# A perceiver block on one core: the context tile's conversion stands behind the key eviction, and the key norm's product behind the next slot's first key products

## The chip, the cores and the metric

The kernel runs on one core of a Trainium2 chip. A core has five engines, each with its own in-order instruction stream: TensorE (PE, matrix products into PSUM), VectorE (DVE), ScalarE (ACT), GpSimd (POOL) and SyncE (SP, which only issues DMAs here). ScalarE also issues DMAs, in the order of its own stream. The metric is the device time in microseconds of one execution. The kernel before took 2119.9 us (median of three runs, 2117.38 to 2125.94).

## What is computed

Eight sequences of 64 tokens with 512 features attend to themselves and, in a cross attention, to a context of 1601 rows of 512 features each. Then follow a sparse attention over the 64 tokens and a feed-forward layer with ternary weights. The change touches the cross attention, whose part of the reference is:

```python
kvx = jnp.einsum('bsi,oi->bso', cond, w_kv_x)          # cond: (8, 1601, 512)
kx, vx = jnp.split(kvx, 2, axis=-1)
kx = _ln(kx.reshape(b, sc, g, d), kxln_w, kxln_b)      # 8 groups, d = 128
vx = vx.reshape(b, sc, g, d)
xout = _gqa(qx, kx, vx).reshape(b, s, nh * d)          # softmax(q k / sqrt(d)) v
```

Keys are thus a product of the context with a weight, normalised over the 128 features of each group and each context row.

## The kernel before

The cross attention is cut into 16 works: 8 sequences times 2 halves of the key groups (4 groups each). A work's context of 1601 rows is cut into 13 tiles of 128 rows (the last has 65), and the tiles into 6 chunks, of two tiles each and the last of three. One turn of the main loop (line 1208, variable g) is a slot. It does a step for one tile in each of several stages, which lag behind each other: a tile is loaded and converted at slot g, its chunk's keys are made 2 slots later (KEYS), the inverse norms are fetched 4 slots later (SPREAD), the scores are made 5 later (SCORES), and probabilities and the weighted sum of the context about 20 later (LAG). So while one work is weighed, the next one's keys are made. 208 slots hold the whole cross attention; other work (projections, self attention, weights, the sparse attention) is pumped in between as a background, with lower priority.

The code is traced in the order in which Python runs it. A scheduler then sets the order of each engine's stream from priorities (earlier in the program is more urgent) and its own estimate of when operands are ready. `tc.issue_after(x)` adds the condition that whatever the block traces on x's engine stands behind x in that engine's stream. It is an order, not a wait, and touches no other engine.

Products are made in pairs of a rounded part and a rest: hi and lo of every operand, three products each. The steps that matter here, for one slot:

- **turned** (line 556): SP loads a transposed context tile cTr (256 KB, L565); ScalarE converts it to cThi (L569); GpSimd takes the difference to cTlo (L570). An odd last tile (65 rows) gets a zero column first, by a GpSimd memset (L567). cTr shares its three buffers (tag "raw") with cr, the untransposed tile of the weighing stage.
- **keys** (line 572): 24 products kx (L588) for two groups of a chunk, 12 for each; ScalarE evicts them twice, the squares ksq (L595) and the scaled keys kthi (L596); VectorE transposes the squares (ksqt, L598), makes the rest ktlo (L599) and reduces the squares to kms (L600). A chunk's four groups take two slots (three for the last chunk).
- **norm** (line 604), once a chunk: a small product kz (L610) gathers kms over partitions into a PSUM bank; VectorE makes kown (L612) and kxv (L614); GpSimd raises to the power -0.5 (L616); VectorE transposes (krt, L618); SP stores 16 KB to DRAM (keyd, L620).
- **spread** (line 622): ScalarE's queue loads keyd back, broadcast to all partitions, into S (512 KB, 642 KB for the last chunk, L626).
- **scores** (line 628): products of queries and keys (L645) into PSUM, and VectorE multiplies them by S and takes the maximum (L649, written as S and cmx in the profile).
- **probs_t, context, weigh**: transposes pt (L677), their halves phi (ScalarE, L687) and plo (VectorE, L688), the context's halves chi (L717) and clo (L721), and 12 products acc (L740 to L742) into the sums U, which ut evicts at a work's end (L748).

PSUM has three banks of the pool that kz, the scores and pt share ("m"), four for the sums U and one for the background; while the sums run, kx takes its bank from the first pool too.

In the order before, a slot traces `turned` in front of `keys`, so conversion has the higher priority. The norm is traced at the slot's end, and its product stands behind `keyed[0]`, the slot's last key or weighing product:

```python
        if 0 <= gK < NA and LAST[kK]:
            with tc.issue_after(keyed[0].ins):
                work[nK].norm(JOBS[kK][0])
```

Of the kernel before, what the change touches and what calls it, by code (L numbers as in the profile page):

```python
# [16 lines left out]
AF = mybir.ActivationFunctionType  # L17
# [4 lines left out]
P = 128  # L22
H = 512
NIC = 4
# [37 lines left out]
def tile_perceiver(ctx: ExitStack, tc: tile.TileContext, t: dict):  # L62
    nc = tc.nc
    V, A, GP, PE = nc.vector, nc.scalar, nc.gpsimd, nc.tensor
# [16 lines left out]
    def nm(s):  # L81
        uid[0] += 1
        return f"{s}_{uid[0]}"

    def ctile(shape, dt, tag):
        return const.tile(shape, dt, tag=tag, name=tag)

    def sm(tag, k=1, dt=F32, bufs=None):
        kw = {} if bufs is None else {"bufs": bufs}
        return small.tile([P, k], dt, tag=tag, name=nm(tag), **kw)  # L90
# [8 lines left out]
    def kxp(tag="kx"):  # L99


        if lane["late"] is not None:
            return lane["late"]
        return accp(tag) if lane["wide"] else mainp(tag)

    def accp(tag="acc"):
        return pacc.tile([P, 512], F32, tag="acc", name=nm(tag))
# [32 lines left out]
    def v3(ap, g):  # L140
        return ap.rearrange("p (g k) -> p g k", g=g)
# [4 lines left out]
    class Late:  # L146
# [13 lines left out]
        ps = staticmethod(lambda tag="b": kxp())  # L160
# [67 lines left out]
    zeros = ctile([P, 1], F32, "zeros")  # L228
# [36 lines left out]
    hw = {"qx": qwb[:, 0:1], "q": qwb[:, 2:3], "k": at["k_norms"][:, 0:1], "kx": at["k_norms"][:, 2:3]}  # L265
# [262 lines left out]
    paced = [None]  # L528
    keyed = [None]
    turn = [None]  # L530
    pin = [None]

    class Cross:
# [22 lines left out]
        def turned(self, tt):  # L556

            t0, n = TT[tt]
            ci = CHUNK_OF[tt]
            o = t0 - TT[CHUNKS[ci][0]][0]  # L560
            if ci not in self.ct:
                self.ct[ci] = [mp.tile([P, NIC, CTW], F32R, tag=x, name=nm(x), bufs=2) for x in ("cThi", "cTlo")]
            chi, clo = self.ct[ci]
            raw = mp.tile([P, NIC, P], F32, tag="raw", name=nm("cTr"), bufs=3)
            paced[0] = nc.sync.dma_start(raw[:, :, :n], t["ctxT"][self.b].rearrange("(c p) k -> p c k", p=P)[:, :, t0:t0 + n])  # L565
            if n & 1:
                GP.memset(raw[:, :, n:n + 1], 0.0)  # L567
                n += 1
            A.copy(chi[:, :, o:o + n], raw[:, :, :n])  # L569
            GP.tensor_tensor(clo[:, :, o:o + n], raw[:, :, :n], chi[:, :, o:o + n].bitcast(F32), ALU.subtract)  # L570

        def keys(self, ci, gs):

            cw = sum(TT[tt][1] for tt in CHUNKS[ci])
            N = cw + (cw & 1)
            nj = (N + 31) // 32
            W = nj * 32
            chi, clo = self.ct[ci]
            if ci not in self.kt:
                self.kt[ci] = [mp.tile([P, HG, KTW], F32R, tag="kt" + x, name=nm("kt" + x), bufs=2) for x in ("hi", "lo")]  # L580
                self.ms[ci] = sm("kms", HG * NRM, bufs=2)
            hi, lo = self.kt[ci]
            ps = kxp()
            for i, g in enumerate(gs):
                k = 0
                for st, mv in ((self.wk[0], chi), (self.wk[1], chi), (self.wk[0], clo)):
                    for ic in range(NIC):
                        self.mm = PE.matmul(ps[:, i * N:(i + 1) * N], lhsT=st[:, ic, g * P:(g + 1) * P], rhs=mv[:, ic, :N], start=k == 0, stop=k == 11)  # L588
                        k += 1
            g0, g1, ng = gs[0], gs[-1] + 1, len(gs)  # L590
            sq = mp.tile([P, 512], F32, tag="kn", name=nm("ksq"), bufs=3)
            if W > N:
                for i in range(ng):
                    A.copy(sq[:, i * W + N:(i + 1) * W], zeros.to_broadcast([P, W - N]))
            A.activation(v3(sq[:, :ng * W], ng)[:, :, :N], v3(ps[:, :ng * N], ng), AF.Square, scale=1.0 / math.sqrt(D))  # L595
            turn[0] = A.activation(hi[:, g0:g1, :N], v3(ps[:, :ng * N], ng), AF.Copy, scale=hw["kx"])  # L596
            sqt = mp.tile([P, 512], F32, tag="kn", name=nm("ksqt"), bufs=3)
            V.transpose(sqt[:, :ng * W], sq[:, :ng * W])  # L598
            V.scalar_tensor_tensor(lo[:, g0:g1, :N], v3(ps[:, :ng * N], ng), hw["kx"], hi[:, g0:g1, :N].bitcast(F32), ALU.mult, ALU.subtract)  # L599
            pin[0] = V.tensor_reduce(self.ms[ci][:, g0 * nj:g1 * nj], sqt[:, :ng * W].rearrange("p (x a) -> p x a", a=32), AX.X, ALU.add)  # L600
            if g1 == HG:
                self.ct.pop(ci)
# [122 lines left out]
        def weigh(self, tt):  # L725

            t0, n = TT[tt]
            if tt == 0:
                self.U = [accp() for _ in range(NIC)]
            phi, plo = self.pp.pop(tt)  # L730
            chi, clo = self.cc.pop(tt)
            last = tt == len(TT) - 1
            for ic in range(NIC):
                s = slice(ic * P, (ic + 1) * P)
                if last:

                    PE.matmul(self.U[ic], lhsT=chi[:, s], rhs=phi, start=False, stop=False)
                    PE.matmul(self.U[ic], lhsT=clo[:S + 3, s], rhs=plo[:S + 3], start=False, stop=True)
                    continue
                PE.matmul(self.U[ic], lhsT=chi[:n, s], rhs=phi[:n], start=tt == 0, stop=False)  # L740
                PE.matmul(self.U[ic], lhsT=chi[:n, s], rhs=plo[:n], start=False, stop=False)  # L741
                keyed[0] = PE.matmul(self.U[ic], lhsT=clo[:n, s], rhs=phi[:n], start=False, stop=False)  # L742

        def weighed(self):
            self.ut = []
# [25 lines left out]
    def last_context():  # L771
        raw = load(mp.tile([P, 512], F32, tag="raw", name=nm("cr"), bufs=3)[:NB], t["ctx"][:, SC - 1, :])
        hi = mp.tile([P, 512], F32R, tag="chi", name=nm("chi"), bufs=2)
        lo = mp.tile([P, 512], F32R, tag="clo", name=nm("clo"), bufs=2)
        A.copy(hi[:NB], raw)
        V.tensor_tensor(lo[:NB], raw, hi[:NB].bitcast(F32), ALU.subtract)
        for b in range(NB):
            for r, x in enumerate((hi, hi, lo)):
                nc.sync.dma_start(codd[b][r:r + 1], x[b:b + 1].bitcast(F32))
# [411 lines left out]
    NT = len(TT)  # L1191
    TURN = {tt: (tt,) for tt in range(NT - 2)}
    TURN[NT - 2] = NT - 2, NT - 1
    JOBS = [(ci, [(2 * i, 2 * i + 1)]) for ci in range(NCH - 1) for i in range(2)]
    LAST = [i % 2 == 1 and i < 2 * (NCH - 1) or i == NT - 1 for i in range(NT)]
    JOBS += [(NCH - 1, x) for x in ([(0,)], [(1,)], [(2,), (3,)])]
    work = [Cross(b, half) for half in range(2) for b in range(NB)]
    NA = NT * len(work)
# [9 lines left out]
    for g in range(NA + LAG + 3):  # L1208
        nA, kA = divmod(g, NT)
        gK = g - KEYS  # L1210
        nK, kK = divmod(gK, NT)
# [36 lines left out]
                    w.exps(0, 0, 2)  # L1248
        if g == LAG - 4:
            last_context()  # L1250
        if g < NA:
            for tt in TURN.get(kA, ()):
                work[nA].turned(tt)
        if 0 <= gK < NA:
            ci, gs = JOBS[kK]
            for x in gs:
                work[nK].keys(ci, x)
            keyed[0] = work[nK].mm
        if g == 0:
            bgA.pump(ALL)  # L1260
        if g == 2:
# [33 lines left out]
        if 0 <= e < NA:  # L1295
            nE, kE = divmod(e, NT)
            work[nE].weigh(kE)
            if kE == NT - 1:
                work[nE].weighed()
        if 0 <= gK < NA and LAST[kK]:  # L1300
            with tc.issue_after(keyed[0].ins):
                work[nK].norm(JOBS[kK][0])
        for bg, q in ((bgA, PACE[g >= LATER]), (bgC, PACE[1]), (bgB, TERNARY_PACE if g < NA + FFN_AT else 0)):
            n = int((g + 1) * q) - int(g * q)

# [81 lines left out]
```

## Time and profile before

| what | value |
|---|---|
| median of three runs | 2119.9 us |
| profiled execution, whole | 2135.21 us |
| its span, first to last instruction | 2133.4 us |
| granted TensorE clock, mean | 0.952 |
| DMA, mean over the span | 190 GB/s |
| TensorE busy 150 to 600 / 600 to 1200 / 1200 to 1800 us | 422.51 / 551.39 / 557.23 us |
| VectorE busy in the same stretches | 336.91 / 409.34 / 372.83 us |
| ScalarE busy in the same stretches | 274.13 / 294.90 / 295.71 us |
| key products (L588), all three kinds | 4608, of some 290 ns each as recorded |
| weighing products (L740 to L742) | 2304, of some 400 ns each as recorded |
| conversions cThi (L569) / differences cTlo (L570) | 208 of 622 / 1195 ns (medians) |

Products overlap: one is recorded with its fill and drain, and the next begins before it ends, so a busy time is a union and the mean of one is longer than its share. A wait is told as the engine's idle time just before an instruction, with the one whose end released it. In the timeline each row has the start, the duration, the engine and line, what is written and read, and in brackets an idle time before it.

### The profile page before, as it was taken

Reading aid. Unit: us, or ns where it says so; the run is one execution under the profiler, and the core shown is the slowest. Engines: PE = TensorE matmul, PEld = TensorE weight load, DVE = VectorE, ACT = ScalarE, POOL = GpSimd, SP = SyncE. Lnnn points to the kernel's source line nnn. Section 1 sums busy time; section 2 is a strip of 40 time slices with the busy share of each in tenths; the row PEclk is TensorE's granted clock in tenths of the full one; section 3 lists DMA queues with packets and bytes.
Section 4 is the critical chain, followed back from the end, with each engine's and each line's share of the span. In section 5 each row is a group of like instructions: output and inputs, shape, how many; then the busy total and the mean of one; then the engine's idle time right before and its main releaser. Section 6 shows DMA issues by size and latency. Waiting matters only on the chain. (4 is left out here: it accounts for less than half of the span.)

```text
span 2133.4 us, 35936 instructions
## 1 busy us (share of the span) xinstructions
PE 1931.0 (91%) x12181; PEld 1702.1 (80%) x12181; DVE 1410.9 (66%) x3769; ACT 1107.7 (52%) x2612; POOL 563.3 (26%) x503
## 2 busy tenths in 40 slices
PE   5789999998999899998989999999989989997998
PEld 5678888888988788887878888888778778874766
DVE  7768787767787577676665556566674765565465
ACT  5456656555655455454434444445644644454554
POOL 5232323322222222212121222222232222210132
PEclk9789999999999999999999999999999999998989
DMA  6566575676565665788776676778556535572425
GB/s 194 141 175 191 153 198 160 194 244 188 161 189 155 209 206 167 226 261 263 246 230 224 218 255 211 250 214 274 170 160 202 163 115 165 157 228 83 142 72 166
DMA packets 361032, 406.31 MB, mean 190 GB/s; under 512 B 45696, under 2 KB 255744, under 8 KB 360848
## 3 DMA queue, kind: packets, MB, share of 16 engines
q1 hardware_dynamic: 310160, 351.54, 51.6%
q10 hardware_dynamic: 50688, 52.47, 10.4%
q8 instruction: 96, 1.57, 0.3%
q14 instruction: 88, 0.72, 0.1%
HBM read 336.40 MB, written 67.26 MB: 189 GB/s over the span
## 5 line engine op out<-in xcount | busy, mean ns | idle before, releaser
L570 POOL TENSOR_TENSOR cTlo<-cTr,cThi 128x512 fp32r<-128x512 f32 (+1 forms) x208 | 251.1, 1215 | 988.6 <-ACT cThi L569 856.9
L741 PE MATMUL acc<-plo,chi 128*128 128x512 f32 x768 | 306.6, 401 | 0.3 <-DVE plo L688 0.3
L742 PE MATMUL acc<-phi,clo 128*128 128x512 f32 x768 | 303.1, 397 | 0.2 <-DMA clo<-clod 0.2
L598 DVE STREAM_TRANSPOSE ksqt<-ksq 128x512 f32<-128x512 f32 (+1 forms) x224 | 147.8, 660 | 220.2 <-ACT ksq L595 219.6
L588 PE MATMUL kx<-cThi,wkhi 128*128 128x256 f32 (+1 forms) x1536 | 274.2, 299 | 5.8 <-DVE m1y L458 2.6
L588 PE MATMUL kx<-cThi,wklo 128*128 128x256 f32 (+1 forms) x1536 | 262.5, 292 | 0.0
L588 PE MATMUL kx<-cTlo,wkhi 128*128 128x256 f32 (+1 forms) x1536 | 261.4, 290 | 0.0
L740 PE MATMUL acc<-phi,chi 128*128 128x512 f32 x768 | 236.2, 412 | 18.8 <-ACT phi L687 18.6
L595 ACT ACTIVATE ksq<-kx 128x512 f32<-128x512 f32 (+1 forms) x224 | 123.7, 552 | 240.9 <-PE kx L588 235.5
L588 PEld LDWEIGHTS kx<-cThi,wkhi 128*128 128x128 f32 x1536 | 230.9, 196 | 21.7 <-DVE m1y L458 3.9
L569 ACT CAST cThi<-cTr 128x512 fp32r<-128x512 f32 (+1 forms) x208 | 122.8, 606 | 220.5 <-DMA cTr<-in_ctxT 145.1
L588 PEld LDWEIGHTS kx<-cThi,wklo 128*128 128x128 f32 x1536 | 224.3, 195 | 4.4 <-issue 3.3
L588 PEld LDWEIGHTS kx<-cTlo,wkhi 128*128 128x128 f32 x1536 | 221.6, 193 | 2.1 <-issue 0.8
L616 POOL TENSOR_TENSOR spread<-kxv,mhalf 128x8 f32<-128x8 f32 x96 | 172.0, 1792 | 185.3 <-DVE kxv L614 162.1
L665 ACT ACTIVATE S<-S,cnm 128x256 f32<-128x256 f32 (+1 forms) x384 | 196.7, 519 | 43.7 <-DVE cnm L660 43.7
L649 DVE CUSTOM_DVE_ANT_0 S<-s,S 128x256 f32<-128x256 f32 (+1 forms) x384 | 152.0, 427 | 68.7 <-DMA S<-keyd 36.5
L717 ACT CAST chi<-cr 128x512 fp32r<-128x512 f32 x192 | 119.1, 620 | 143.5 <-PE acc L741 82.5
L740 PEld LDWEIGHTS acc<-phi,chi 128*128 128x128 f32 x768 | 140.1, 195 | 47.7 <-ACT phi L687 23.7
L741 PEld LDWEIGHTS acc<-plo,chi 128*128 128x128 f32 x768 | 146.5, 191 | 30.2 <-issue 3.5
L742 PEld LDWEIGHTS acc<-phi,clo 128*128 128x128 f32 x768 | 145.7, 190 | 27.4 <-issue 0.8
L688 DVE TENSOR_TENSOR plo<-pt,phi 128x512 fp32r<-128x512 f32 x192 | 131.2, 684 | 53.1 <-ACT phi L687 52.2
L687 ACT CAST phi<-pt 128x512 fp32r<-128x512 f32 x192 | 112.5, 587 | 92.4 <-PE pt L677 92.0
(350 smaller groups left out, 3731.3 us busy)
## 6 DMA issues: line engine op xcount, KB each, us to landing
cTr<-in_ctxT SPq DMA_DIRECT2D x192, 256.0 KB
cr<-in_ctx SPq DMA_DIRECT2D x192, 256.0 KB
ws<-wpd SPq DMA_DIRECT2D x88, 512.0 KB
S<-keyd ACTq DMA_DIRECT2D x80, 512.0 KB
clod<-clo SPq DMA_DIRECT2D x96, 256.0 KB
clo<-clod SPq DMA_DIRECT2D x96, 256.0 KB
wv<-in_wkv SPq DMA_DIRECT2D x64, 256.0 KB
tern<-in_ffn_w SPq DMA_DIRECT2D x64, 256.0 KB
```

What stands on the lines that cost most here:

```text
L569: A.copy(chi[:, :, o:o + n], raw[:, :, :n])
L570: GP.tensor_tensor(clo[:, :, o:o + n], raw[:, :, :n], chi[:, :, o:o + n].bitcast(F32), ALU.subtract)
L588: self.mm = PE.matmul(ps[:, i * N:(i + 1) * N], lhsT=st[:, ic, g * P:(g + 1) * P], rhs=mv[:, ic, :N], start=k == 0, stop=k == 11)
L595: A.activation(v3(sq[:, :ng * W], ng)[:, :, :N], v3(ps[:, :ng * N], ng), AF.Square, scale=1.0 / math.sqrt(D))
L598: V.transpose(sqt[:, :ng * W], sq[:, :ng * W])
L616: GP.tensor_tensor(r[:, :nj], v[:, :nj], mhalf[:, :nj], ALU.pow)
L649: V.tensor_tensor_reduce(sc[:, g, :cw], ps[:, :cw], sc[:, g, :cw], 1.0, -3.0e38, ALU.mult, ALU.max, self.mx[:, g * NCH + ci:g * NCH + ci + 1])
L665: A.activation(self.S[ci][:, g, :cw], self.S[ci][:, g, :cw], AF.Exp, bias=self.nmx[:, g:g + 1], accum_out=self.su[:, g * NCH + ci:g * NCH ...
L688: V.tensor_tensor(lo[:n], pt[:n], hi[:n].bitcast(F32), ALU.subtract)
L740: PE.matmul(self.U[ic], lhsT=chi[:n, s], rhs=phi[:n], start=tt == 0, stop=False)
L741: PE.matmul(self.U[ic], lhsT=chi[:n, s], rhs=plo[:n], start=False, stop=False)
L742: keyed[0] = PE.matmul(self.U[ic], lhsT=clo[:n, s], rhs=phi[:n], start=False, stop=False)
```

## The change

Three things change. The zero column of an odd tile is written by ScalarE as a copy of a zero tile. `turned` is traced behind `keys` and the norm, and its ScalarE instructions stand behind `keyt[0]`, the slot's last key eviction (L596). The norm of a chunk is traced one slot later than before, right behind that slot's keys, and its product stands behind the first 12 of them (the last product of the first group); the weighing products no longer set `keyed[0]`.

```diff
             if n & 1:
-                GP.memset(raw[:, :, n:n + 1], 0.0)
+                A.copy(raw[:, :, n:n + 1], zeros.unsqueeze(1).to_broadcast([P, NIC, 1]))
...
-                        self.mm = PE.matmul(ps[:, i * N:(i + 1) * N], ...)
+                        mm = PE.matmul(ps[:, i * N:(i + 1) * N], ...)
                         k += 1
+                if i == 0:
+                    keyed[0] = mm
...
-            turn[0] = A.activation(hi[:, g0:g1, :N], v3(ps[:, :ng * N], ng), AF.Copy, scale=hw["kx"])
+            turn[0] = keyt[0] = A.activation(hi[:, g0:g1, :N], v3(ps[:, :ng * N], ng), AF.Copy, scale=hw["kx"])
...
-                keyed[0] = PE.matmul(self.U[ic], lhsT=clo[:n, s], rhs=phi[:n], start=False, stop=False)
+                PE.matmul(self.U[ic], lhsT=clo[:n, s], rhs=phi[:n], start=False, stop=False)
...
-        if g < NA:
-            for tt in TURN.get(kA, ()):
-                work[nA].turned(tt)
         if 0 <= gK < NA:
             ci, gs = JOBS[kK]
             for x in gs:
                 work[nK].keys(ci, x)
-            keyed[0] = work[nK].mm
+        if 0 <= gK - 1 < NA and LAST[(gK - 1) % NT]:
+            with tc.issue_after(keyed[0].ins):
+                work[(gK - 1) // NT].norm(JOBS[(gK - 1) % NT][0])
+        if g < NA:
+            for tt in TURN.get(kA, ()):
+                with tc.issue_after(keyt[0].ins) if keyt[0] is not None else nullcontext():
+                    work[nA].turned(tt)
...
-        if 0 <= gK < NA and LAST[kK]:
-            with tc.issue_after(keyed[0].ins):
-                work[nK].norm(JOBS[kK][0])
```

More of the change, by code (lines that the diff above doesn't have):

```diff
@@ L530, in tile_perceiver @@
     turn = [None]
+    keyt = [None]
     pin = [None]
@@ L587, in keys @@
                     for ic in range(NIC):
-                        self.mm = PE.matmul(ps[:, i * N:(i + 1) * N], lhsT=st[:, ic, g * P:(g + 1) * P], rhs=mv[:, ic, :N], start=k == 0, stop=k == 11)
+                        mm = PE.matmul(ps[:, i * N:(i + 1) * N], lhsT=st[:, ic, g * P:(g + 1) * P], rhs=mv[:, ic, :N], start=k == 0, stop=k == 11)
                         k += 1
+                if i == 0:
+                    keyed[0] = mm
             g0, g1, ng = gs[0], gs[-1] + 1, len(gs)
```

## The prediction

> **What bounds the kernel now.** I read the head of the page first, then the waits of each engine, then the order of time around one norm.
>
> ```profile
> span 2133.4 us, 35936 instructions
> PE 1931.0 (91%) x12181; PEld 1702.1 (80%) x12181; DVE 1410.9 (66%) x3769; ACT 1107.7 (52%) x2612; POOL 563.3 (26%) x503
> ```
>
> TensorE is busy for 91%; 202 us of the span are its gaps, and a change of order can only fill gaps or open new ones. Between 150 and 1915 us, where the slots run, the gaps sum to 1765 - 1641 = 124 us (busy time by stretches). The waits of all engines say who ended them (total us, times, longest):
>
> ```profile
> PE kz L610 <- DVE kms L600: 44.5, 30, 4.5
> PE acc L740 <- ACT phi L687: 18.6, 14, 3.0
> PE s L645 <- DVE kown L612: 10.2, 7, 3.2
> PE s L645 <- DVE cqb L652: 5.7, 6, 2.6
> ACT cThi L569 <- DMA cTr<-in_ctxT: 145.1, 67, 6.3
> POOL cTlo L570 <- ACT cThi L569: 856.9, 143, 19.4
> DVE S L649 <- DMA S<-keyd: 36.5, 16, 6.8
> ```
>
> The largest gap of TensorE is the norm's small product kz waiting for the reduction kms. The last row is the one to watch: even now the multiply of the scores by the inverse norms (S, L649) waits 16 times for its 512 KB to land. Its chain, in order of time, for one chunk:
>
> ```profile
> 664.24 0.31 PE L610 MATMUL kz<-kms,over 128*128 128x32 f32 x2
> 665.08 0.19 DVE L612 SCALAR_TENSOR_TENSOR kown<-kz,quad 128x32 f32<-128x32 f32 x1
> 665.30 0.22 DVE L614 TENSOR_REDUCE kxv<-kown 128x8 f32<-128x32 f32 x1
> 665.60 1.64 POOL L616 TENSOR_TENSOR spread<-kxv,mhalf 128x8 f32<-128x8 f32 x1 [3.67 <-DVE kxv L614]
> 667.75 0.21 DVE L618 STREAM_TRANSPOSE krt<-spread 128x32 f32<-128x32 f32 x1
> 668.27 0.33 SPq L620 DMA_DIRECT2D keyd<-krt  x1
> 671.86 0.37 ACTq L626 DMA_DIRECT2D S<-keyd  x1
> 678.47 0.42 DVE L649 CUSTOM_DVE_ANT_0 S<-s,S 128x256 f32<-128x256 f32 x1 [0.70 <-DMA S<-keyd]
> ```
>
> From kz to the multiply it is 13.9 us, through five queues, and at the end VectorE stands idle (0.70) until the DMA lands.
>
> **How I measure cover.** The built order of before and after is known, so I count the TensorE work that stands between two places. Prices are the cadence of back-to-back products in the trace: four key products of 256 columns start every 0.47 us (1018.83, 1019.30), so 0.118 each; 0.228 for 512 columns, 0.148 for 322. All products sum to 1846 us of the 1931 busy. I turn such work into time with 1.08, between 1931/1846 = 1.046 and 2133.4/1846 = 1.155.
>
> **The change part by part.**
>
> *The norm moves behind the next slot's first key products.* From the last key product of a chunk to kz there were 4.4 us of work on average, now 10.1, never under 4.1. What kz needs in that time is ksq 0.55, ksqt 0.66, ktlo 0.71, kms 0.67, so about 2.6 us plus queueing; the 30 waits end: -44.5 us (at least -30, if VectorE is late at the tightest places; no more than -44.5). The norm issues seven things: kz on TensorE, kown, kxv and krt on VectorE, the power on GpSimd, the 16 KB store on SP and, two places later, the 512 KB load on ScalarE's queue. All come later, past the next slot's context tile, its probabilities and the scores of the chunk before. On GpSimd the power still stands directly behind a subtraction (67 of 96, before 70), on SP the store behind a context load (37 of 96, before 38): there nothing new.
>
> *ScalarE converts after the key eviction.* The 208 conversions (0.61 each) and their subtractions on GpSimd (1.2) keep their number. Before, 67 of them held ScalarE for 145.1 us until cTr landed; the load now stands 15.0 us of work ahead of its use instead of 8.2, while the other load, cr, falls from 14.3 to 7.5 (they share three buffers). TensorE sees this at phi: places where fewer than 2 us of work cover phi fall from 48 to 18, so 18.6 x 18/48 = 7.0, a gain of 11.6 (bounds 0 and 18.6). Places under 2 us behind kown fall from 47 to 35, now mostly in front of key products: 10.2 x 35/47 = 7.6, gain 2.6, say 3 (0 to 10.2).
>
> *What it uncovers.* From cThi to its first key product 23.9 us of work become 9.3, from cTlo 24.6 become 10.8. 13 key products now have under 2 us behind cThi; at the price of the phi rows, 18.6/48 = 0.39 us each, that is +5. About six find cTlo short of its 0.62 + 1.2 us plus queueing: +3. The eviction of the sums U (ut) has 19 such places, with none before: +6. Together +14, bounds 0 and 40.
>
> *The odd column* is written by ScalarE, not GpSimd: 16 copies of 128x4, nearest row the 128x4 copy of L696, 0.19 to 0.22 us: 3 us of a ScalarE that is idle for 48%. Zero; 3 if uncovered.
>
> *Where the stall goes.* kz is later, the scores are not. From kz to the multiply there were 16.8 us of work, now 8.7; from kz to the first product that waits behind the multiply, less the VectorE work in between, 18.4 become 11.7, or 12.6 us of time. Needed, by the trace's 96 chunks: kz to the issue of the store 5.35 on average (2.81 to 11.10); store to the earliest load 1.8 (least 1.42); load from issue to its last packet 5.56 (4.46 to 9.77); then 0.45. Sum 13.2, the least of each 9.0; the 17 chunks where the multiply waited took 16.2. Summing what is missing over the 96 places gives 137 us for 13.2, 32 for 9.0, 357 for 16.2. The same count on the old order gives 50 for 13.2 where the waits of TensorE behind cmx and cqb show about 14, because a late multiply partly hides under other waits. So 137 is worth between 137 x 14/50 = 38 and 137, less the 14 paid already: +24 to +123. I take +85, nearer the upper end, for this reason: in the old order VectorE had 220 of the 384 multiplies between a kown and its krt, so kown came first; in the new order 298 stand between kms and kown, so kown comes after the previous chunk's multiplies. A multiply that waits now delays the next chain as well; behind it stand also ksqt, ktlo and kms, for which key products wait. On ScalarE the load's issue waits for the store: 5.7 us of work between them become 3.1, and chi, ksq and phi stand behind it, with 8.5 us of work before TensorE asks: +5, bounds 0 and 30.
>
> The Trainium skill, "DMA: Bandwidth & Descriptors", section "Anatomy of one DMA — SWDGE (gpsimd) path", puts a DMA at about 2.0 us fixed plus its bytes at 436 GB/s (a fit for the other kind of queue). Store and load would then take 2.0 + 3.2 = 5.2 us where the rows above say 1.8 + 5.56 = 7.4; by the page the chain is 11 us, the missing cover about 60 instead of 137, and the sum about -15, 2105. The measured load is slower than the page's figure, which is what speaks against this change.
>
> Sum: -44.5 - 11.6 - 3 + 14 + 85 + 5 = +45 us on the span of 2133.4, 2178. That execution took 2135.2 (1.8 around the span), 15.3 above the median 2119.9 of the three shown, so the forecast is 2119.9 + 45 = 2165.
>
> **The rivals.**
> *The chain stays hidden, faster.* For it: ScalarE no longer blocks on cTr, and VectorE is idle for 34%, so it can catch up after a wait. Against it: the 36.5 us of S waits with twice the cover. With the chain at its shortest, 32 - 14 = 18: -59 + 14 + 18 = -27, 2093 (down to 2072 if the new waits cost nothing and the chain 11).
> *Gain and loss cancel.* The chain costs about 40: 2120.
> *The chain decides every chunk.* If it takes the 16.2 us of its bound cases and nothing hides, +343 - 40 = +303, 2423. It needs a loop: late multiply, late kown, late store. The loop needs 16.2 us and 2 for its four multiplies, against 17.9 for two slots (208 slots in the 1862 us from the first to the last key product), so it just closes. Against it: 2.2 of the 16.2 are the load standing in ScalarE's queue past the earliest issue (4.0 on average in those 17 chunks, against 1.8), and that place moves closer.
> *The change does nothing.* Excluded: in the built order kz moved back by 5.7 us of work on average.
>
> **How the numbers follow.** Slower through the chain: 54%, own range 2131 to 2243 (chain +123, new waits +40, gain only -40). The chain decides throughout: 6%. Cancel: 13%. Faster: 27%, 2072 to 2109. About 0.5% (10.6 us) is what a measurement can tell from no change, so faster 0.27, same 0.13, slower 0.60. The likeliest case's time is 2165; for 8 in 10 the range reaches from 2072 to 2243.
>
> **What would show it.** Right: kz behind kms vanishes from TensorE's waits; VectorE's wait of S for its DMA rises from 36.5 to some 200 us and over 50 times; TensorE waits for cmx, cqb, kown or ktlo more than now; ScalarE's wait for cTr falls under 30. Wrong: if the S waits grow and TensorE does not follow, the cover behind the multiply is larger than I count, and the result is near 2093; if the S waits stay under 80 us, kz runs earlier against the scores than the order suggests. A lower granted clock than 0.952 under a denser TensorE would move the time for a reason that is in none of the terms.

## The result, and the profile after

The changed kernel takes 2183.6 us (median of three, 2182.1 to 2193.8) against 2119.9: a ratio of 1.0308, with an interval from 1.0249 to 1.0368. It is slower by 64 us, where the forecast was +45 (2165, range 2072 to 2243). The head of the page after:

```profile
span 2181.9 us, 35769 instructions
PE 1945.4 (89%) x12181; PEld 1699.6 (78%) x12181; DVE 1379.2 (63%) x3769; ACT 1097.9 (50%) x2628; POOL 551.5 (25%) x487
```

The number of products is the same. TensorE's gaps (span less busy time) went from 202 to 236.5 us, its busy time from 1931.0 to 1945.4. The waits of all engines (total us, times, longest) say what ended the new gaps:

```profile
DVE S L652 <- DMA S<-keyd: 286.1, 80, 11.2
ACT chi L720 <- DMA cr<-in_ctx: 158.4, 60, 9.1
PE s L648 <- DVE cqb L655: 25.3, 9, 5.0
PE kx L589 <- DVE cmx L652: 21.7, 8, 5.4
PE kz L613 <- DVE cmx L652: 18.7, 13, 2.6
PE s L648 <- DVE cmx L652: 13.4, 4, 5.0
PE pt L680 <- DVE cmx L652: 7.4, 13, 2.7
PE kx L589 <- DVE kown L615: 7.1, 9, 2.4
PE kx L589 <- ACT cThi L570: 6.0, 6, 1.6
```

The wait of kz for kms, 44.5 us before, is no longer among them. In its place VectorE waits in 80 of 96 chunks for the load of the inverse norms, 286.1 us where it was 36.5, and TensorE waits for what VectorE does after that: five rows, two with cqb and cmx in front of scores, three with cmx in front of key products, kz and transposes, 86.5 us together. Before, the rows with cqb and cmx held 14.2 us in all, 5.7 of them with cqb and the rest with cmx:

```profile
PE s L645 <- DVE cmx L649: 4.9, 2, 3.6
PE sc L476 <- DVE cmx L649: 1.9, 1, 1.9
PE kx L588 <- DVE cmx L649: 1.7, 3, 1.2
```

One chunk shows the mechanism at its worst, in order of time (start, duration, engine and line, operation, and in brackets the idle time before it):

```profile
1384.48 0.30 PE L613 MATMUL kz<-kms,over 128*128 128x32 f32 x2
1387.32 0.17 DVE L615 SCALAR_TENSOR_TENSOR kown<-kz,quad 128x32 f32<-128x32 f32 x1
1389.35 0.20 DVE L617 TENSOR_REDUCE kxv<-kown 128x8 f32<-128x32 f32 x1
1389.62 2.69 POOL L619 TENSOR_TENSOR spread<-kxv,mhalf 128x8 f32<-128x8 f32 x1 [3.04 <-DVE kxv L617]
1392.35 0.21 DVE L621 STREAM_TRANSPOSE krt<-spread 128x32 f32<-128x32 f32 x1 [0.41 <-POOL spread L619]
1392.59 0.33 SPq L623 DMA_DIRECT2D keyd<-krt  x1
1395.02 0.37 ACTq L629 DMA_DIRECT2D S<-keyd  x1
1405.58 0.43 DVE L652 CUSTOM_DVE_ANT_0 S<-s,S 128x256 f32<-128x256 f32 x1 [11.20 <-DMA S<-keyd]
...
1406.41 0.80 PE L589 MATMUL kx<-cThi,wkhi 128*128 128x256 f32 x2 [5.38 <-DVE cmx L652]
```

kown starts 2.5 us after kz has ended, because VectorE had other work, and kxv 2 us later. The load's last packet lands at 1405.08, 10.1 us after its issue. VectorE has been idle for 11.20 us when it may multiply, and TensorE for 5.38. Averaged over the 96 chunks, the trace gives for the pieces of the chain, before and after: end of kz to the store's issue 5.35 and 5.07 us, store to load 4.74 and 2.79, load issue to last packet 5.56 and 6.19, last packet to the multiply 4.77 and 0.63, in all 20.4 and 14.7. What the change took out is mostly slack: 4.1 us between the landing and the multiply, and 2.0 us that the load stood behind the store's issue (at least 1.42 in both). In the chain of work that ended last (shares of the span by engine, then by line) the load is the largest item, 16%, and its store adds 5%. Before, that chain could be followed back over only a tenth of the span, so e3 below is what it is to be compared with.

```profile
PE 43%; DMA 32%; DVE 13%; ACT 6%; issue 4%; POOL 2%; SPq 1%; DVEq 0%; ACTq 0%; POOLq 0%
DMA S<-keyd 16%; PE kx L589 15%; DMA keyd<-krt 5%; PE acc L743 3%; PE acc L744 3%; PE acc L745 3%; PE s L648 3%; DMA cr<-in_ctx 2%; DVE S L652 2%; PE pt L680 2%; PE xo L764 2%; PE pj L353 2%; DMA wv<-in_wkv 2%; PE pp L444 2%; DMA ws<-wpd 1%
```

### The profile page after: what moved, and what is told of

Its sections match the earlier page's. It is cut to its first block, busy times and chain, and to the rows that moved or that the text cites. A ratio compares the mean times of both kernels' runs of the same rounds, so it can differ in the third digit from the quotient of the medians.

```text
span 2181.9 us, 35769 instructions
## 1 busy us (share of the span) xinstructions
PE 1945.4 (89%) x12181; PEld 1699.6 (78%) x12181; DVE 1379.2 (63%) x3769; ACT 1097.9 (50%) x2628; POOL 551.5 (25%) x487
## 4 chain that ended last, share of the span: by engine, by line
PE 43%; DMA 32%; DVE 13%; ACT 6%; issue 4%; POOL 2%; SPq 1%; DVEq 0%; ACTq 0%; POOLq 0%
DMA S<-keyd 16%; PE kx L589 15%; DMA keyd<-krt 5%; PE acc L743 3%; PE acc L744 3%; PE acc L745 3%; PE s L648 3%; DMA cr<-in_ctx 2%; DVE S L652 2%; PE pt L680 2%; PE xo L764 2%; PE pj L353 2%; DMA wv<-in_wkv 2%; PE pp L444 2%; DMA ws<-wpd 1%
## 5 line engine op out<-in xcount | busy, mean ns | idle before, releaser
L571 POOL TENSOR_TENSOR cTlo<-cTr,cThi 128x512 fp32r<-128x512 f32 (+1 forms) x208 | 242.7, 1168 | 503.7 <-ACT cThi L570 473.5
L652 DVE CUSTOM_DVE_ANT_0 S<-s,S 128x256 f32<-128x256 f32 (+1 forms) x384 | 151.0, 430 | 295.8 <-DMA S<-keyd 286.1
L589 PE MATMUL kx<-cThi,wkhi 128*128 128x256 f32 (+1 forms) x1536 | 282.7, 307 | 49.5 <-DVE cmx L652 21.7
L589 PE MATMUL kx<-cThi,wklo 128*128 128x256 f32 (+1 forms) x1536 | 269.9, 298 | 0.0
L589 PE MATMUL kx<-cTlo,wkhi 128*128 128x256 f32 (+1 forms) x1536 | 266.4, 295 | 0.7 <-POOL cTlo L571 0.7
L743 PE MATMUL acc<-phi,chi 128*128 128x512 f32 x768 | 256.2, 411 | 6.9 <-ACT chi L720 3.4
L720 ACT CAST chi<-cr 128x512 fp32r<-128x512 f32 x192 | 119.1, 620 | 237.2 <-DMA cr<-in_ctx 158.4
L589 PEld LDWEIGHTS kx<-cThi,wklo 128*128 128x128 f32 x1536 | 232.3, 201 | 2.7 <-issue 1.6
L589 PEld LDWEIGHTS kx<-cTlo,wkhi 128*128 128x128 f32 x1536 | 227.4, 197 | 5.6 <-issue 1.6
L668 ACT ACTIVATE S<-S,cnm 128x256 f32<-128x256 f32 (+1 forms) x384 | 197.1, 522 | 36.7 <-DVE cnm L663 36.5
L680 PE MATMUL pt<-ident,S 128*128 128x128 f32 (+1 forms) x832 | 141.3, 282 | 12.0 <-DVE cmx L652 7.4
L602 DVE SCALAR_TENSOR_TENSOR ktlo<-kx,cols,kthi 128x512 fp32r<-128x512 f32 (+1 forms) x224 | 147.9, 660 | 0.2 <-ACT kthi L599 0.2
```

The costliest lines, as they stand in the source:

```text
L652: V.tensor_tensor_reduce(sc[:, g, :cw], ps[:, :cw], sc[:, g, :cw], 1.0, -3.0e38, ALU.mult, ALU.max, self.mx[:, g * NCH + ci:g * NCH + ci + 1])
L668: A.activation(self.S[ci][:, g, :cw], self.S[ci][:, g, :cw], AF.Exp, bias=self.nmx[:, g:g + 1], accum_out=self.su[:, g * NCH + ci:g * NCH ...
L680: PE.transpose(pt[:n, g * P:(g + 1) * P], self.S[ci][:, g, o:o + n], ident)
```

## The experiments

Theory A: the chain from kz to the multiply is no longer covered. B: ScalarE's new order, with the conversion behind the eviction, costs the time. C: the new order as a whole does, whatever S waits for. The kernel before took 2128.3, 2130.3 and 2129.8 us in the three groups of runs; where ratios are turned into us below, 1% is 21.3 us.

| run | edit | median us | ratio to before | interval |
|---|---|---|---|---|
| | the change | 2183.6 | 1.0308 | 1.0249 to 1.0368 |
| e1 | norm's move alone | 2171.3 | 1.0193 | 1.0165 to 1.0220 |
| e2 | conversion's move alone | 2117.0 | 0.9935 | 0.9905 to 0.9966 |
| e3 | the change, S from older norms | 2032.9 | 0.9543 | 0.9521 to 0.9565 |
| e4 | before, S from older norms | 2118.8 | 0.9943 | 0.9915 to 0.9971 |
| e5 | the change, norm ahead of the keys | 2118.8 | 0.9957 | 0.9931 to 0.9983 |
| e6 | the change, load of S in two | 2131.9 | 0.9990 | 0.9966 to 1.0015 |
| e7 | e5 and e6 together | 2082.3 | 0.9778 | 0.9741 to 0.9815 |
| e8 | the change, power twice | 2341.4 | 1.0984 | 1.0921 to 1.1046 |
| e9 | e1, S from older norms | 2027.5 | 0.9529 | 0.9484 to 0.9575 |
| e10 | e2, S from older norms | 2102.6 | 0.9872 | 0.9836 to 0.9908 |
| e11 | before, power twice | 2155.7 | 1.0127 | 1.0079 to 1.0176 |
| e12 | e2, load of S in two | 2092.4 | 0.9829 | 0.9787 to 0.9870 |

**Each part alone.** e1 is the kernel before with the norm's part of the diff: keyed[0] set after the first group's products, the weighing no longer setting it, and norm traced one slot later behind the keys. e2 is the other part:

```diff
 # e1: in part
             for x in gs:
                 work[nK].keys(ci, x)
-            keyed[0] = work[nK].mm
+        if 0 <= gK - 1 < NA and LAST[(gK - 1) % NT]:
+            with tc.issue_after(keyed[0].ins):
+                work[(gK - 1) // NT].norm(JOBS[(gK - 1) % NT][0])
...
-        if 0 <= gK < NA and LAST[kK]:
-            with tc.issue_after(keyed[0].ins):
-                work[nK].norm(JOBS[kK][0])
 # e2: in part
-                GP.memset(raw[:, :, n:n + 1], 0.0)
+                A.copy(raw[:, :, n:n + 1], zeros.unsqueeze(1).to_broadcast([P, NIC, 1]))
...
+                with tc.issue_after(keyt[0].ins) if keyt[0] is not None else nullcontext():
                     work[nA].turned(tt)
```

> The kernel before with the norm's move alone; the conversion stays in front of the keys. Theory A (the inverse norms' chain kz, power, store, load is too late for the score multiply): 2150 to 2195 us, the multiply's wait for the load S over 200 us in total, TensorE's wait of kz for kms under 8 us. Theory B (the loss is the conversion's late place and the context loads that come late with it): 2070 to 2115 us, because the 44.5 us at kz are gone and the conversion is as before.

> The kernel before with the conversion's move alone (and the zero column on ScalarE); the norm stays at the slot's end. Theory A: 2100 to 2140 us, the multiply's wait for S under 80 us. Theory B: 2150 to 2190 us, with chi waiting over 100 us for cr.

The norm's move alone makes the kernel slower by 1.9%, the conversion's move alone makes it faster by 0.65%. So B falls. In the waits of e1 the row to read is again that of S:

```profile
DVE S L651 <- DMA S<-keyd: 298.0, 88, 8.5
```

The two ratios multiply to 1.0127, not 1.0308; e9 and e10 come back to that.

**The chain taken away.** In e3 and e4 the load of S fetches the inverse norms that the work before stored, so no multiply has to wait for its own chain (the first of the 16 works excepted). All instructions and transfers remain, but the scores are scaled by other norms than the reference's.

```diff
-            nc.scalar.dma_start(self.S[ci][:, :, :cw], keyd[(self.b + self.half * NB) % 2][ci][:, :cw].partition_broadcast(P))
+            nc.scalar.dma_start(self.S[ci][:, :, :cw], keyd[(self.b + self.half * NB + (self.b + self.half > 0)) % 2][ci][:, :cw].partition_broadcast(P))
```

> The changed kernel, but S is loaded from the inverse norms that the work before stored, so that the load need not wait for this chunk's norm; every instruction is still there, the scores are scaled by other norms. Theory A: faster than the kernel before, 2060 to 2110 us, the multiply's wait for S under 30 us. Theory B: 2150 us or more. A third theory, C (the scheduler's new order as a whole is worse, no single chain): 2140 us or more.

> The same on the kernel before: S from the norms of the work before. Theories A and B: 2085 to 2120 us, since only 36.5 us of S waits are there to go, and few of them reach TensorE. If it gains as much as the changed kernel does from the same edit, the chain was no more binding after the change than before it, and theory A falls.

The changed kernel falls to 2032.9 us, 151 us below itself; the kernel before falls by 0.57%, 12 us. e3 is faster than A expected (2060 to 2110), e4 within its band. The waits of e3 have S near where it was before the change, though above the 30 us that were expected:

```profile
DVE S L652 <- DMA S<-keyd: 45.6, 24, 5.5
```

In its chain of work that ended last the load of S has 2% where the changed kernel has 16%, and TensorE 64% instead of 43%:

```profile
PE 64%; DMA 19%; DVE 9%; ACT 4%; issue 2%; SPq 1%; POOL 1%; ACTq 0%; POOLq 0%; DVEq 0%
PE kx L589 20%; PE acc L744 6%; PE acc L743 6%; PE acc L745 6%; PE s L648 5%; DMA cr<-in_ctx 5%; DMA ws<-wpd 4%; PE pj L353 3%; PE pt L680 3%; DMA S<-keyd 2%; PE xo L764 2%; PE pp L444 2%; PE p L872 1%; DMA wpd<-ws 1%; DMA ld<-in_wproj 1%
```

This speaks for A and against C: without its chain the new order is the faster one by 4.0% (0.9543 against 0.9943, plus or minus 0.4%). But e3 does not take the waiting alone away. With the dependence gone the scheduler also builds another order: in the two traces 2628 of the 12181 products stand outside the longest order that e3 and the changed kernel have in common, against 246 for e4 and the kernel before. Around the norm the two orders agree (counted with the prediction's prices, 10.2 us of TensorE work from a chunk's last key product to kz in both, and from kz to the chunk's first score product 6.9 in e3 and 6.7). How much of the 151 us belongs to the rest of the order is not shown. For A speak besides e3 the waits of the changed kernel, and the runs that follow.

**The chain lengthened.** If A holds, a microsecond added to each chain must come out in the changed kernel, and not in the old one. e8 and e11 issue GpSimd's power twice, in the changed kernel and in the kernel before.

```diff
             GP.tensor_tensor(r[:, :nj], v[:, :nj], mhalf[:, :nj], ALU.pow)
+            GP.tensor_tensor(r[:, :nj], v[:, :nj], mhalf[:, :nj], ALU.pow)
```

> The changed kernel with GpSimd's power between kxv and krt issued twice, 1.64 us more in the chain of each of the 96 chunks; the output stays the same. Theory A: the chain already decides in most chunks, so most of 96 x 1.64 = 157 us comes on top: +95 to +150, 2275 to 2335. Rival (the loss comes from kz's place or ScalarE's order, with the chain hidden): within +20, as GpSimd is busy 25% of the span.

> The old kernel with GpSimd's power issued twice, 1.64 us more in the chain of each of the 96 chunks, as was done to the changed kernel, where it cost 158 us of the 157 that 96 x 1.64 makes; the output stays the same. Theory A (in the old order cover of 18.4 us hides the chain): a few chunks with the least cover pay, S wait 36.5 to about 60, ratio 1.002 to 1.015. Rival (the power costs in any order, for example as GpSimd delays cTlo and clo for which TensorE waits): ratio 1.04 or more.

The changed kernel pays 144 us by the ratios (1.0984 less 1.0308, plus or minus 0.9%), or 158 by the plain medians; the kernel before pays 27 (1.27%). The median of e8 is just above the expected band, that of e11 within it. Both expectations count with 96 times 1.64 us, 157, but the traces show that more was added. From the start of the first power to the end of the last, e8 takes 4.30 us on average where the changed kernel takes 1.76, and e11 4.01 where the kernel before takes 1.79, since in 55 and 24 of the 96 chunks other GpSimd work, mostly a subtraction, stands between the two powers. So 2.5 us were added to each chain in e8, 244 in all, and 2.2 us in e11, 213 in all; the changed kernel pays 0.6 of them and the kernel before an eighth. This is a price, not a count of chunks, because an idle TensorE costs more than the idle time (last section). The count stands in the waits of S: 93 of 96 chunks in e8, 26 in e11. e8 first:

```profile
DVE S L653 <- DMA S<-keyd: 419.0, 93, 10.7
```

```profile
DVE S L650 <- DMA S<-keyd: 60.2, 26, 4.5
```

**Cover given back, chain shortened.** e5 places the norm in the same slot ahead of the keys, tied to no product. e6 issues S as two loads of two groups each. e7 does both. e12 puts the two loads into e2, whose norm is at its old place.

```diff
 # e5: norm ahead of the keys
+        if 0 <= gK - 1 < NA and LAST[(gK - 1) % NT]:
+            work[(gK - 1) // NT].norm(JOBS[(gK - 1) % NT][0])
         if 0 <= gK < NA:
             ci, gs = JOBS[kK]
             for x in gs:
                 work[nK].keys(ci, x)
-        if 0 <= gK - 1 < NA and LAST[(gK - 1) % NT]:
-            with tc.issue_after(keyed[0].ins):
-                work[(gK - 1) // NT].norm(JOBS[(gK - 1) % NT][0])
 # e6: two loads
-            nc.scalar.dma_start(self.S[ci][:, :, :cw], keyd[(self.b + self.half * NB) % 2][ci][:, :cw].partition_broadcast(P))
+            for h in range(0, HG, 2):
+                nc.scalar.dma_start(self.S[ci][:, h:h + 2, :cw], keyd[(self.b + self.half * NB) % 2][ci][h:h + 2, :cw].partition_broadcast(P))
```

> The changed kernel with the norm ahead of that slot's key products instead of behind the first of them, and tied to no product; everything else as changed. In the built order kz still has 7.2 us of TensorE work behind the last key product of its chunk (least 2.2; 4.4 before the change, 10.1 after it), and the cover from kz to the first product behind the multiply, less VectorE's work, is 13.9 us against 11.7 in the changed kernel and 18.4 in the old. Theory A (the chain from kz to the multiply lacks cover): the missing cover falls by the share that 2.2 of 6.7 us makes, so about a third to a half of the 150 us that the chain cost by the run with the norms of the work before: 2085 (2060 to 2120), and VectorE's wait of S for its load falls from 286 to some 130 us. Rival (the order around the norm costs as a whole, or the tie to the first key product sets the loss): 2170 or more, or a fall of the time at the same wait for S.

> The changed kernel with the 512 KB load S issued as two loads of two groups each on the same queue; its order else unchanged. Theory A with the load's transfer time as a main part of the chain: the first multiply can start when half has landed, so the chain is shorter by up to 2 us of 14.7 for the first two groups, 2100 (2080 to 2150), S wait 286 to about 180. Rival (the load's fixed time and its place in ScalarE's queue are what is late, and a second issue costs ScalarE 0.4 us more each): 2175 or more, S wait 260 or more.

> Both of the last two edits on the changed kernel. Theory A: the two add, as both give the same chain cover: 2050 (2035 to 2080), near the 2033 of the run with the norms of the work before, S wait under 80; it would beat the kernel before. Rival (loss is not cover): no better than the better of the two alone.

> The conversion's move and the zero column on the old kernel, norm at its old place, and the load S issued as two loads of two groups each. It tells whether the kernel with the norm ahead of the next keys and the split load (ratio 0.9778) gains by the norm's place or by the split alone. Theory A (the norm's place gives back the wait of kz for kms, 48 us in the conversion's move alone): the split alone finds little left to hide here, S wait 36 to about 15, ratio 0.985 to 0.993. Rival (the gain is the split's): ratio 0.98 or less.

Waits of S in e5, e6 and e7, in this order:

```profile
DVE S L652 <- DMA S<-keyd: 112.1, 48, 6.7
```

```profile
DVE S L653 <- DMA S<-keyd: 240.0, 96, 8.2
```

```profile
DVE S L653 <- DMA S<-keyd: 59.2, 44, 4.7
```

e5 takes 3.5 points off the ratio of 1.0308, e6 3.2, both together 5.3; all three rivals fall. The sizes were missed: e5 is at the far edge of its band and e7 just outside. In e6 VectorE's wait fell only to 240.0, not to some 180. By the trace, half of the load's packets have landed 3.7 us after the first issue (mean), against 6.2 for the whole load in the changed kernel (where half had landed as early, at 3.4 us, but the multiply waits for all of it), and kz to the first multiply falls from 14.7 to 13.4 us; but of the 240 us, 40 now stand in front of the third multiply, which needs the second half. The Trainium skill, "Perfetto Trace Analysis", section "DMA Optimizations", both advises larger transfers and says that splitting may let some start sooner; here the second holds, as the first half is all that the first two multiplies need.

e7 beats the kernel before by 2.2%. e12 shows that most of this can be had from the two loads and the conversion's move alone: with the norm at its old place they reach 1.7%, and the intervals of e7 and e12 overlap. e12 lies between its two expectations, so what the norm's place adds by itself, 0.5%, is not settled.

**Where the parts interact.** e9 and e10 take the chain away from each part alone, with the edit of e3, and complete the square.

> The old kernel with the norm's move alone, and S loaded from the norms that the work before stored, so that no multiply waits for its own chain; the scores are scaled by other norms than the reference's. It tells where the two parts of the change interact: alone they gave ratios of 1.0193 and 0.9935, together 1.0308 instead of 1.0127, about 38 us. Theory I (the interaction sits in the chain: with the conversion moved as well, VectorE and ScalarE fall behind a late multiply more): without the chain the parts add, before 2119, conversion -14, so this kernel is the fully changed one without its chain, 2033, plus about 14: 2045 (2035 to 2060), and the chain costs about 125 in the norm's move alone against 150 in the whole change. Rival II (the chain costs the same in both; the moved conversion loses where it gained, as key products stand right behind it once the norm is gone from there): 2020 (2005 to 2030), below the changed kernel without its chain.

> The old kernel with the conversion's move and the zero column alone, and S loaded from the norms that the work before stored, so that no multiply waits for its own chain; the scores are scaled by other norms than the reference's. Fourth corner of the same square. If the chain is hidden at the norm's old place whatever the conversion does, as the old kernel's own pair says (0.9943 with the same edit), it is near the conversion's move alone: 2105 (2095 to 2117). If the chain already costs this kernel much, below 2085.

| ratio to before | own norms | older norms | so the chain costs |
|---|---|---|---|
| before | 1 | 0.9943 | 0.6% |
| conversion moved | 0.9935 | 0.9872 | 0.6% |
| norm moved | 1.0193 | 0.9529 | 6.6% |
| both | 1.0308 | 0.9543 | 7.7% |

e9 came out at 2027.5 us, in the band of rival II, and not at 2045: without the chain the norm's move alone is already as fast as the whole change. e10 came out as expected, near e2. So the conversion's move gains 0.7% beside the old norm and nothing (0.1%, plus or minus 0.5%) beside the late one. That is about half of the 1.8% by which the parts do not add. The other half would be the chain's higher cost in the whole change, 7.7 against 6.6%; with intervals of 0.6% on the ratio of the change this is not resolved, and stays open. It also depends on the kernel before of the first three runs, 2119.9 us, beside which alone the changed kernel ran: by plain medians the chain costs 151 us in the whole change and 144 in the norm's move alone, and the parts miss by 24 us, 1.1%.

## Why the prediction was nearly right, and where it was not

**The place and the mechanism: right.** What was to show it came: kz behind kms vanished, VectorE's wait of S went to 286 us and 80 times (some 200 and over 50 were expected), TensorE waits more for cmx, cqb and ktlo (not for kown, which the list also had), and ScalarE's wait for cTr fell from 145.1 to 3.7 us for the conversions. The waits together with e3 and e5 to e8 show the chain as the cause; its exact share of the loss is open, as said at e3. The fit in the Trainium skill, "DMA: Bandwidth & Descriptors", section "Anatomy of one DMA — SWDGE (gpsimd) path", by which the sum would have been 2105, made store and load 5.2 us together; the load alone took 6.19 in the changed kernel, and the measurement decides.

**The gain of the norm's move, -44.5: right as a wait, half of the gain.** The prediction counted the wait of kz for kms alone. Without the chain the move is worth 0.9529 less 0.9943, -4.1% or -88 us (plus or minus 11), with the other order that the scheduler then builds. The waits of e4, and under them those of e9, have the kz row as forecast and the phi row with it:

```profile
PE kz L610 <- DVE kms L600: 51.4, 31, 5.6
PE acc L740 <- ACT phi L687: 15.0, 11, 2.6
```

```profile
PE kz L612 <- DVE kms L602: 3.9, 1, 3.9
PE acc L742 <- ACT phi L689: 2.1, 3, 1.0
```

From single profiles (us):

| | span | TensorE busy | gaps | time at half clock | of it TensorE busy |
|---|---|---|---|---|---|
| e4, before without chain | 2126.9 | 1912.9 | 214.0 | 174.1 | 133.1 |
| e9, norm moved without chain | 2022.1 | 1875.3 | 146.8 | 94.0 | 63.7 |
| e3, the change without chain | 2027.3 | 1885.3 | 142.0 | 102.4 | 83.6 |
| the change | 2181.9 | 1945.4 | 236.5 | 189.2 | 162.9 |

From e4 to e9 the gaps fall by 67 us, 60 of them by the two rows above, and the busy time by another 38 for the same products. In the kernel before, key products of 256 columns start every 0.119 us at full clock and every 0.213 at half, 1.8 times as far apart. So the 69 us less of busy time at half clock explain some 31 of the 38.

**The chain, +85: mis-sized in the same way.** Measured as what the chain costs more than in the old order, it is 7.7 less 0.6%, or 151 us, by ratios, and 151 - 12 = 139 by medians: above the upper bound of 123. In the profiles, from e3 to the change, the gaps rise by 94.5 us, close to the 85, and the busy time by 60.1. By the same working the 79 us more of busy time at half clock explain 35 of the 60; the other 25 are not explained. From e4 to the kernel before the gaps differ by 12 us the other way, so single profiles give these sizes to some 10 us at best. The estimate of gaps was good; what it left out is that a product after a gap is slow. The step that failed is the prediction's sentence that a change of order can only fill gaps or open new ones: here it moved the busy time as well. No term of the sum had this, though the profile of before gave a mean clock of 0.952.

**Two errors that nearly cancel.** Without the chain the forecast's terms make 45 - 85 = -40; the measured difference is 0.9543 less 0.9943, -85 us (plus or minus 8). Both sides were low, in good part by the same omission, and between the kernel before and the change, where the time at half clock hardly moved (205 and 189 us), the omission nearly cancels. That 45 came out near 64 is thus partly luck.

**The phi term, -11.6: given to the wrong part.** The wait of acc for phi, 18.6 us before, is down to 1.1 us in the change. But in e2, with the conversion's move alone, it is 22.0 us, and in e1, with the norm's move alone, 3.3. The rows of the change, e2 and e1, in this order:

```profile
PE acc L743 <- ACT phi L690: 1.1, 3, 0.6
```

```profile
PE acc L741 <- ACT phi L688: 22.0, 20, 3.3
```

```profile
PE acc L742 <- ACT phi L689: 3.3, 5, 1.0
```

The count of covered places was made on the order of the whole change and put down to the conversion. What the conversion's move gains beside the old norm, 14 us, is not in this row; its profile has 205 - 151 = 54 us less time at half clock than that of the kernel before, with nearly the same gaps (205 and 202 us). Why was not tried.

**The small terms.** The waits for cThi came to 6.0 us (+5 forecast). The zero column's 16 copies took 0.2 us each, and only one row of 0.5 us in all names them: nothing, as said. That ScalarE stands behind cr for 158.4 us instead of cTr for 145.1 costs nothing that shows: e9 waits 143.3 us for cTr and e3 187.7 for cr, and their times are 2027.5 and 2032.9. S's issue on ScalarE, +5, was not separated: rows of ScalarE waiting for the store grew from 7 to 24 us.

**The rivals.** "The chain stays hidden" gave 2093; with the chain really gone it is 2033, so this rival's gain was too small as well, for the reason above; but the case did not come. "The chain decides every chunk" gave 2423. VectorE does wait for the load in 80 of 96 chunks, and in 93 in e8; but that the loop (late multiply, late kown, late store) closes is not shown, since e8 pays 144 of the 244 us added. Its price was too high, since it took the 16.2 us of the worst 17 chunks for all (the wait row has 16), where the end of kz to the multiply came to 14.7.

## What to carry to other kernels

A wait of the busiest engine can be removed by moving its producer later, but everything that hangs on that producer moves too: count the cover of the whole chain to its last consumer, DMAs included, and compare it with the measured length before moving. Test a suspected chain twice: feed its consumer with something older, and lengthen it by a piece. Where a scheduler sets the order, look in the traces how far either edit changed the order too, and by how much the chain really grew. Before undoing an order, try to shorten the chain (here by loading in two parts): e7, with the norm moved less far and two loads, is 2.2% faster than the kernel before. Whether the norm's move adds to that is open, as e12 without it is 1.7% faster.

## What the runs showed of the hardware

A TensorE gap costs more than its length. The trace records the granted clock as 1.0 or 0.5; at a gap, or soon behind it, it falls to 0.5 for 3.4 or 6.8 us, rarely longer. In the changed kernel, by stretches (window, length, busy time of PE, PEld, DVE, ACT and POOL with instructions, granted clock, DMA share, GB/s):

```profile
815.00:818.60 3.60, 3.60 (x23) 3.07 (x22) 0.00 (x0) 0.38 (x2) 0.00 (x0) 1.00 0.93 259
818.60:821.10 2.50, 0.05 (x2) 0.02 (x1) 0.85 (x5) 0.58 (x3) 0.00 (x0) 1.00 0.68 236
822.00:825.20 3.20, 3.20 (x14) 3.06 (x14) 2.49 (x12) 1.11 (x3) 1.01 (x1) 0.50 0.00 0
825.30:830.00 4.70, 4.70 (x37) 4.48 (x36) 3.90 (x11) 4.46 (x15) 1.51 (x3) 1.00 0.37 115
```

A gap of 2.5 us at full clock is followed, 0.9 us later, by 3.2 us in which 14 products run at clock 0.50, where the stretches on both sides, at 1.00, ran 23 in 3.6 us and 37 in 4.7 (their shapes are mixed). Between 150 and 1915 us, of the gaps of 2 us or more, 20 of 23 in the kernel before had the clock at 0.5 at their end or within 6 us of it, 19 of 22 in the changed one, 12 of 17 in e1, 38 of 43 in e8 and 7 of 8 in e3; every one of the 27 and 26 stretches of the first two had at least 1 us of idle time in the 7 us ahead of it. The Trainium skill, "TensorE: Matmul & The Clock Gate", section "Why this matters for your kernels", advises to avoid gaps longer than about 3 us; these runs agree that the clock falls to half, but it did so at 36 of the 44 gaps of only 2 to 2.5 us in these five runs, where other idle time can stand close by.

A load's length goes with what else the DMA engines carry: the same 512 KB took 4.60 to 10.06 us from issue to last packet in the changed kernel. The quarter of the 80 loads with the least other traffic in the 5 us after the issue (24 GB/s) took 5.53 us on average, the quarter with the most (193 GB/s) 7.07. The 10.06 is that of the chunk shown above; in the 5 us after its issue the DMA engines were busy all the time:

```profile
1395.00:1400.00 5.00, 5.00 (x38) 4.68 (x37) 0.00 (x0) 0.62 (x1) 0.00 (x0) 1.00 1.00 278
```
